# Triangle attention followed by a window scan: score, bias and maximum in one VectorE operation, and a projection in another PSUM bank

## The chip, the cores and the metric

The kernel runs on one core of a Trainium2 chip. The metric is the device time of one execution in microseconds (us); a lower time is better. The engines of the core work from queues of their own, each in order, and wait for each other by semaphores: TensorE (PE: matrix products and transposes, results into PSUM), VectorE (DVE), ScalarE (ACT), GpSimd (POOL) and SyncE (SP: issues the DMAs). SBUF and PSUM are the on-chip memories[...].

## The reference

Two layers work on an image of 256 x 256 positions with 128 channels, in float32. Each is added to its own input: `x = x + layer(group_norm(x))`. Layer 1 (convolution, windowed selective scan, gated projection) is not edited here. Layer 0 is attention along each of the 256 rows, with four heads of 32 channels:

```python
xn = (x - mu) * jax.lax.rsqrt(var + EPS) * ln_w + ln_b
tri_bias = jnp.einsum('bijd,dh->bhij', xn, w_tri)[:, None]
mask_bias = INF * (mask[:, :, None, None, :] - 1.0)
q = (xn @ w_q).reshape(B, I, J, H, C) * (1.0 / np.sqrt(C))
...
scores = jnp.einsum('bimhc,binhc->bihmn', q, k) + tri_bias + mask_bias
attn = jax.nn.softmax(scores, axis=-1)
o = jnp.einsum('bihmn,binhc->bimhc', attn, v)
g = jax.nn.sigmoid((xn @ w_g + b_g).reshape(B, I, J, H, C))
o = (g * o).reshape(B, I, J, H * C)
return o @ w_o + b_o
```

For every row and head the scores are a 256 x 256 matrix: a product of queries and keys plus a bias that is the same for all rows (tri_bias) plus a mask bias.

## The kernel before

The program has three stretches. The first computes statistics and normalised input (`xn_d`) and the bias `tri_d`. The second is the attention loop. The third is layer 1: a scan with its own schedule, which begins with `group_norm(1)` and so needs the statistics of all pairs of the second.

The attention loop takes the rows in 128 pairs of 512 tokens. One step of the loop is one row; even and odd steps alternate, and the order of all work in a step is written out by hand (under a manual schedule, L553 to L641), so the order of these calls is the order of each engine's queue. In step s the loop works on several rows at once:

- `now` (row s): its scores, made in the step before, get their bias and maximum and are exponentiated.
- `mid` (row s-2): its exponentials are transposed on PE (`turn`), 128 x 128 at a time, and copied out of PSUM (`turn_out`), one head by VectorE, one by ScalarE.
- `old` (row s-3): its transposed exponentials meet the values in `mix`, giving o_p.
- `nxt` (row s+1): its scores are computed by PE.
- pairs `ahead`, `behind`, `done`: queries, keys and values of the next pair; gate and softmax shares of the last; output projection of the one before that.

What each name does, with its engine:

- `scores` (L455 to L468, PE): sc0 and sc1, two PSUM tiles of two banks each, one for two heads. A tile has four blocks of 128 x 256: two heads by two halves of the query positions.
- `bias` (L446, GpSimd): tm, tri bias plus mask, 128 x 2048 per row, two steps ahead.
- `add` (L470, VectorE): `at` = scores + tm for the four blocks of a tile at once, 128 x 1024.
- `peak` (L478, VectorE): nmax, the negative maximum of each block, over 128 x 1024.
- `exps` (L484, ScalarE): `exp(at + nmax)` in place, one operation per block, its sums into den.
- `invert` and `widen` (L496, L500): the reciprocals of den (VectorE), spread out by GpSimd.
- `queries`, `keys`, `values`, `gates`, `shares`, `project`: PE products into the one-bank tile that `side0` (L337) hands out, tag m. The pool has one such buffer, so a product waits until the one before it has been read out.
- `queries_out` (L366), `keys_out` (L374), `values_out` (L389): read out on ScalarE. `gates_out` (L397), `shares_out` (L415), `project_out` (L426): on VectorE. The last writes xr, which `store` (L431) puts into the statistics and sends to memory.
- `gather` (L418, VectorE): og, the product of o_p with the gate.
- o_p (L535) has a PSUM bank of its own. sc0 and sc1 take four banks, the transposes two, tag m one, o_p one[...].

`logistic` (L129) is the sigmoid of the gate, three ScalarE operations, each on the last one's result.

Of the kernel before, what the change touches and what calls it, by code (L numbers as in the profile page):

```python
# [12 lines left out]
F32 = mybir.dt.float32  # L13
AF = mybir.ActivationFunctionType
ALU = mybir.AluOpType
AX = mybir.AxisListType
# [3 lines left out]
P = 128  # L20
# [4 lines left out]
HC = 32  # L25
# [42 lines left out]
def kernel(  # L68
# [28 lines left out]
    nc = tc.nc  # L97
# [31 lines left out]
    def logistic(e):  # L129

        nc.scalar.activation(e, e, AF.Exp, scale=-1.0)
        nc.scalar.activation(e, e, AF.Ln, bias=one)
        nc.scalar.activation(e, e, AF.Exp, scale=-1.0)
# [34 lines left out]
    for dh in range(2):  # L168
        nc.scalar.dma_start(
            out=wtap[:, dh], in_=conv_w[:, dh * P : (dh + 1) * P].rearrange("t d -> d t")  # L170
# [5 lines left out]
    for dh in range(2):  # L176
        for k in range(KD):
            o, back = k % 2, k // 2
            for at, lo, n in (
# [5 lines left out]
                    out=wx[:, dh, o, at : at + n],  # L185
# [4 lines left out]
    for back in range(2):  # L190
        at = 32 * back
        nc.scalar.dma_start(
            out=wdt[at : at + DTR], in_=dt_w[:, 2 * back : 2 * back + 2]
        )
        for o in range(2):
            for dh in range(2):
                j = 2 * (o + 2 * back) + dh
                nc.scalar.dma_start(
                    out=wdt[at + DTR : at + DTR + 1, o, dh * P : (dh + 1) * P],
# [61 lines left out]
    with tc.tile_pool(name="lnc", bufs=1) as cp, tc.tile_pool(  # L261
        name="lnx", bufs=3
    ) as xp, tc.tile_pool(name="lnt", bufs=3) as tp, tc.tile_pool(
        name="lnp", bufs=2, space=PSUM
# [9 lines left out]
        for k in range(KD):  # L274
            for nh in range(2):
                for blk in range(NBLK):
                    nc.scalar.dma_start(
                        out=bdiag[k][nh][blk].rearrange("p t n -> p (t n)"), in_=zero
# [33 lines left out]
    with tc.tile_pool(name="atc", bufs=1) as cp, tc.tile_pool(  # L312
        name="atx", bufs=7
    ) as xp, tc.tile_pool(name="att", bufs=3) as tp, tc.tile_pool(
        name="ats", bufs=8
    ) as wp, tc.tile_pool(name="atps", bufs=1, space=PSUM) as ps_s, tc.tile_pool(
        name="atpt", bufs=1, space=PSUM
    ) as ps_t, tc.tile_pool(name="atpm", bufs=1, space=PSUM) as ps_m, tc.tile_pool(
        name="atpo", bufs=1, space=PSUM
# [11 lines left out]
        for mc in range(2):  # L331
            nc.sync.dma_start(
                out=trib[:, :, mc, :],
# [3 lines left out]
        def side0(name):  # L337
            return ps_m.tile([P, 512], F32, name=name, tag="m")

        class Pair:  # L340
# [24 lines left out]

            def queries_out(self):  # L366
                self.qs = tp.tile([P, 512], F32, name="qs")
                nc.scalar.mul(self.qs, self.q_p, 1.0 / math.sqrt(HC))

            def keys(self):  # L370
                self.k_p = side0("k_p")
# [48 lines left out]
                nc.vector.tensor_mul(self.og, self.o_p, self.gate)  # L420

            def project(self):
                self.y_p = side0("y_p")
                nc.tensor.matmul(self.y_p, wo, self.og, start=True, stop=True)

            def project_out(self):  # L426
# [8 lines left out]
        class Row:  # L435
# [32 lines left out]
                        )  # L468

            def add(self, hp):  # L470
                self.at[hp] = wp.tile([P, 4, IMG], F32, name="at")
                nc.vector.tensor_add(  # L472
                    self.at[hp],
                    self.sc[hp].rearrange("p h m n -> p (h m) n"),
                    self.tm[:, 4 * hp : 4 * hp + 4],
                )

            def peak(self, hp):  # L478
                self.nmax[hp] = wp.tile([P, 4], F32, name="nmax")
                nc.vector.tensor_reduce(  # L480
                    self.nmax[hp], self.at[hp], AX.X, ALU.max, negate=True
                )

            def exps(self, hp, js):  # L484
                if hp == 0 and js[0] == 0:
                    self.den = wp.tile([P, NH, 2], F32, name="den")
                for j in js:
                    nc.scalar.activation(  # L488
                        self.at[hp][:, j, :],
                        self.at[hp][:, j, :],  # L490
                        AF.Exp,
                        bias=self.nmax[hp][:, j : j + 1],
                        accum_out=self.den[:, 2 * hp + j // 2, j % 2 : j % 2 + 1],
                    )

# [36 lines left out]
            def mix(self):  # L532
                pair = self.pair
                if self.r == 0:
                    pair.o_p = ps_o.tile([P, 512], F32, name="o_p")  # L535
                for n in range(2):
                    for h in range(NH):
                        base = h * HC
                        nc.tensor.matmul(
                            pair.o_p[base : base + HC, self.row],  # L540
                            pair.vs[:, self.r, n, base : base + HC],
                            self.aT[h][:, n, :],
                            start=(n == 0),
                            stop=(n == 1),
                        )
# [4 lines left out]
        def pick(items, i):  # L550
            return items[i] if 0 <= i < len(items) else None

        with tc.manual_schedule():  # L553
            for pair in pairs[0:4]:
                pair.load()
            first = pairs[0]
            first.mask_bias()
            rows[0].bias()
            rows[1].bias()
            first.queries()  # L560
            first.queries_out()
            first.keys()
            first.keys_out()
            rows[0].scores()
            first.values()
            first.values_out()
            for s in range(n_rows + 4):
                sg, odd = divmod(s, 2)
                now, nxt, mid, old = (
                    pick(rows, s),  # L570
                    pick(rows, s + 1),
                    pick(rows, s - 2),
                    pick(rows, s - 3),
                )
                ahead, behind, done = (
                    pick(pairs, sg + 1),
                    pick(pairs, sg - 1),
                    pick(pairs, sg - 2),
                )
                if not odd:  # L580
                    if sg + 4 < n_pairs:
                        pairs[sg + 4].load()
                    if behind:
                        behind.load_residual()
                    if ahead:
                        ahead.mask_bias()
                if s + 2 < n_rows:
                    rows[s + 2].bias()
                if old:
                    old.mix()  # L590
                if now:
                    now.add(0)
                    now.peak(0)
                if mid:
                    mid.turn(0)
                if now:
                    now.exps(0, [0])
                if done:
                    if odd:
                        done.project_out()  # L600
                    else:
                        done.gather()
                if mid:
                    mid.turn_out(0)
                if now:
                    now.exps(0, [1, 2, 3])
                if odd and ahead:
                    ahead.keys()
                    ahead.keys_out()
                if not odd and behind:  # L610
                    behind.gates()
                    behind.gates_out()
                if now:
                    now.add(1)
                if mid:
                    mid.turn(1)
                    mid.turn_out(1)
                if now:
                    now.peak(1)
                if odd and behind:  # L620
                    behind.shares()
                    behind.shares_out()
                if not odd and ahead:
                    ahead.queries()
                    ahead.queries_out()
                if now:
                    now.exps(1, [0, 1, 2, 3])
                if nxt:
                    nxt.scores()
                if odd and ahead:  # L630
                    ahead.values()
                    ahead.values_out()
                if not odd and done:
                    done.project()
                if odd and done:
                    done.store()
                if not odd and behind:
                    logistic(behind.gate)
                if 0 <= s - 1 < n_rows:
                    rows[s - 1].invert()  # L640
                    rows[s - 1].widen()  # L641
# [648 lines left out]
    with tc.manual_schedule():  # L1290
# [37 lines left out]
        for i, unit in enumerate(units):  # L1328
            j, place = divmod(i, per_job)
# [102 lines left out]
```

## Time and profile before

| | |
|---|---|
| median of 3 runs | 24110.36 us (24109.98 to 24111.08) |
| profiled execution, device time | 24104.07 us |
| its span, first to last instruction | 24102.3 us |
| granted TensorE clock, mean | 0.993 |
| instructions | 423533 |
| PE, VectorE, ScalarE, GpSimd busy | 95%, 91%, 77%, 88% of the span |
| first and last sum of scores and bias (L472) | 541.6 and 2718.0 us |

The busy shares are means over the whole span, and most of that is layer 1, so they say little of the attention loop, which lies between about 541 and 2720 us. In groups of instructions, a row gives source line, engine, operation, the tiles written and read (buffer numbers left out), their shapes and the count; behind the bar the busy time in us and the mean duration of one in ns; behind the second bar the engine's idle time just before them and what ended most of it. Busy time counts overlapping instructions once, so it can be less than the count times the mean. In a table of waits, a row gives who waited, for whom, the total in us, how many times, and the longest. In a timeline, a row gives the start, the length, engine, line and operation. Matrix products are pipelined and their ends are modelled.

### The profile page before, as it was taken

What the parts mean: (1) busy time and instruction counts of PE and PEld (TensorE: products, weight loads), DVE (VectorE), ACT (ScalarE), POOL (GpSimd) and SP (SyncE); (2) the same over time, 40 slices, a digit from 0 to 9 for tenths busy, and PEclk for the clock granted to TensorE, in tenths of its full rate; (3) what the DMA queues carried; (4) which work ended last, traced back from release to release, by engine and by line L of the source; (5) the groups of instructions that cost most, each with busy time, mean ns of one, the idle gap of its engine ahead of it and who ended that gap; (6) DMA issues with size and microseconds to landing.
All of it is one profiled execution on the core that took longest, in us unless ns stands there. A gap on an engine that the chain in (4) does not pass through costs nothing.

```text
span 24102.3 us, 423533 instructions
## 1 busy us (share of the span) xinstructions
PE 22947.3 (95%) x171020; PEld 17081.0 (71%) x171020; DVE 22036.1 (91%) x14740; ACT 18625.8 (77%) x35334; POOL 21291.6 (88%) x5966
## 2 busy tenths in 40 slices
PE   7888899999999999999999999999999999999999
PEld 2555577777777777777777777777777777777777
DVE  6888899999999999999999999999999999999998
ACT  5777777777777777777777777777777777777776
POOL 3666699999999999999999999999999999999999
PEclk9999999999999999999999999999999999999999
DMA  5222244444444444444444444444444444444444
GB/s 195 64 62 62 93 159 160 157 159 161 159 160 158 159 160 160 160 158 159 160 161 159 159 158 160 160 160 160 158 159 160 160 160 158 159 160 160 160 159 147
DMA packets 2000298, 3638.51 MB, mean 151 GB/s; under 512 B 1129584, under 2 KB 1131760, under 8 KB 1725824
## 3 DMA queue, kind: packets, MB, share of 16 engines
q1 hardware_dynamic: 1985616, 3602.35, 43.4%
q8 instruction: 1346, 22.05, 0.4%
q10 hardware_dynamic: 12720, 9.07, 0.1%
q14 instruction: 616, 5.05, 0.1%
HBM read 3467.33 MB, written 143.65 MB: 150 GB/s over the span
## 4 chain that ended last, share of the span: by engine, by line
PE 60%; DVE 23%; issue 7%; ACT 7%; DMA 2%; SPq 1%; POOL 0%; ACTq 0%; POOLq 0%; DVEq 0%
PE b_p L1180 22%; PE y_p L1218 19%; DVE h L1200 18%; PE dt_p L1017 4%; PE cv_p L768 4%; ACT at L488 2%; PE xd_p L948 2%; PE dut_p L1051 2%; PE in_p L719 1%; ACT da L1167 1%; DMA res<-x_d 1%; PE sc L462 1%; DVE dt L1033 1%; PE v_p L381 1%; DVE nmax L480 1%
## 5 line engine op out<-in xcount | busy, mean ns | idle before, releaser
L1207 POOL TENSOR_TENSOR h<-h,cc 128x2048 f32<-128x2048 f32 x4096 | 18591.8, 4549 | 1460.5 <-POOL h L1207 544.8
L1200 DVE TENSOR_TENSOR_SCAN h<-da,b_p 128x1024 f32<-128x1024 f32 x8192 | 18228.9, 2270 | 1417.8 <-PE b_p L1180 1384.6
L1167 ACT ACTIVATE da<-dt,am 128x508 f32<-128x508 f32 x16384 | 10396.2, 706 | 1236.5 <-DVE h L1200 1223.9
L1180 PE MATMUL b_p<-diag,dut 64*128 64x256 f32 x65536 | 8594.4, 395 | 622.9 <-DVE h L1200 559.3
L1218 PEld LDWEIGHTS y_p<-ident,h 128*128 128x128 f32 x65536 | 7141.4, 140 | 1412.9 <-issue 1386.7
L1218 PE MATMUL y_p<-ident,h 128*128 128x128 f32 x65536 | 8003.9, 275 | 5.9 <-POOL h L1207 5.9
L1180 PEld LDWEIGHTS b_p<-diag,dut 64*128 64x128 f32 x65536 | 5852.3, 186 | 2946.7 <-DVE h L1200 1353.8
L736 ACT ACTIVATE tap<-xin,wtap 128x512 f32<-128x512 f32 x2048 | 1432.3, 743 | 0.0
L1040 POOL TENSOR_TENSOR du<-dt,u 128x512 f32<-128x512 f32 x1024 | 1307.4, 1277 | 58.9 <-DMA z<-bt 56.0
L768 PE MATMUL cv_p<-ident,tap 128*128 128x128 f32 x9216 | 1225.6, 274 | 5.1 <-DVE xct L785 3.7
L1158 ACT ACTIVATE da<-ident 128x16 f32<-128x16 f32 x1536 | 347.9, 227 | 1140.8 <-DVE h L1200 1140.8
L488 ACT ACTIVATE at<-at,nmax 128x256 f32<-128x256 f32 x2048 | 1019.4, 502 | 237.8 <-DVE nmax L480 237.8
L449 POOL TENSOR_TENSOR tm<-trib,mb 128x2048 f32<-128x2048 f32 x256 | 1166.3, 4556 | 10.7
L768 PEld LDWEIGHTS cv_p<-ident,tap 128*128 128x128 f32 x9216 | 1047.6, 141 | 170.1 <-issue 161.5
L1027 ACT ACTIVATE sp<-dt_p 128x512 f32<-128x512 f32 x1024 | 602.4, 588 | 728.3 <-PE dt_p L1017 728.2
L1017 PE MATMUL dt_p<-xd,wdt 9*128 9x512 f32 x2048 | 1151.1, 641 | 2.5 <-DVE dt L1033 2.2
L1060 ACT COPY dut<-dut_p 128x512 f32<-128x512 f32 x1024 | 586.6, 573 | 473.0 <-PE dut_p L1051 473.0
L503 POOL COPY wide<-rden 128x256 f32<-128x256 f32 x256 | 101.5, 396 | 826.8 <-DVE rden L498 824.9
L1028 ACT ACTIVATE sp<-sp,one 128x512 f32<-128x512 f32 x1024 | 743.0, 726 | 33.4
L516 PEld LDWEIGHTS aT_p<-ident,at 128*128 128x128 f32 x4096 | 451.0, 141 | 343.0 <-issue 142.6
L1033 DVE SCALAR_TENSOR_TENSOR dt<-sp,dt_p 128x512 f32<-128x512 f32 x1024 | 677.8, 662 | 16.0 <-DMA z<-bt 11.3
L472 DVE TENSOR_TENSOR at<-sc,tm 128x1024 f32<-128x1024 f32 x512 | 613.5, 1198 | 56.5 <-POOL wide L503 30.8
(132 smaller groups left out, 16368.0 us busy)
## 6 DMA issues: line engine op xcount, KB each, us to landing
cc<-c_d SPq DMA_DIRECT2D x2048, 1024.0 KB
diag<-z SPq DMA_DIRECT2D x1024, 1024.0 KB
xt<-in_x_dram SPq DMA_DIRECT2D x16, 2048.0 KB
xt<-in_x_dram SPq DMA_DIRECT2D x32, 1024.0 KB
xn_d<-xn SPq DMA_DIRECT2D x32, 1024.0 KB
xn<-xn_d SPq DMA_DIRECT2D x128, 256.0 KB
mb<-in_mask_dram SPq DMA_DIRECT2D x128, 256.0 KB
xr<-in_x_dram SPq DMA_DIRECT2D x128, 256.0 KB
```

The source lines that it names most:

```text
L449: nc.gpsimd.tensor_add(self.tm, trib.rearrange("p h m n -> p (h m) n"), self.pair.mb[:, self.row].unsqueeze(1).to_broadcast([P, 2 * NH, IMG]),
L488: nc.scalar.activation(self.at[hp][:, j, :], self.at[hp][:, j, :], AF.Exp, bias=self.nmax[hp][:, j : j + 1], accum_out=self.den[:, 2 * hp ...
L736: nc.scalar.activation(scaled.rearrange("p s (y x) -> p s y x", x=WIN), self.xin[:, dh] .rearrange("p y f x -> p (y f) x")[:, 2 * dy : 2 * ...
L768: nc.tensor.matmul(cv_p[:, s], one_tap[:, s], ident, start=(t == 0 and s == 0), stop=(t == 8 and s == GS - 1), is_transpose=True, skip_gro ...
L1017: nc.tensor.matmul(token_order(self.dt_p), wdt[rows, self.o, dh * P : (dh + 1) * P], token_blocks(self.xd[rows]), start=True, stop=True,)
L1033: nc.vector.scalar_tensor_tensor(dt, self.sp, CEIL, self.dt_p, ALU.min, ALU.max)
L1040: nc.gpsimd.tensor_mul(token_blocks(du), token_order(self.dt[back][dh]), token_blocks(self.u[:, dh]),)
L1167: nc.scalar.activation(da[:, :, j, lo:hi], dt[:, :, lo:hi], AF.Exp, scale=am[:, a0 : a0 + 1])
L1180: nc.tensor.matmul(b_p[:, s, :, h * 64 : (h + 1) * 64].rearrange("p n t -> p t n"), job.dut[self.back][rows, p, h, self.dh * P : (self.dh ...
L1200: nc.vector.tensor_tensor_scan(out=out_, data0=d0, data1=d1, initial=0.0, op0=ALU.mult, op1=ALU.add)
L1207: nc.gpsimd.tensor_mul(self.pair, self.pair, cc.rearrange("p n s t -> p s n t"))
L1218: nc.tensor.matmul(job.y_p[:, 2 * p + s, self.dh * P : (self.dh + 1) * P], self.h[:, s, j], ident, start=(first and s == 0 and j == 0), st ...
```

## The change

Six edits, all in the attention loop:

1. `add` and `peak` become one. Instead of a 128 x 1024 addition and a 128 x 1024 reduction for each tile, four `tensor_tensor_reduce` operations per tile each handle one 128 x 256 block: they write at = -(scores + tm) and fold the minimum of it into the block's column of nmax. In the compiled order each is two VectorE instructions, one of 128 x 256 and one that writes 128 x 1. `peak` is gone, and nmax of sc1 is made where `add(1)` stood, ahead of the second transposes' copy.
2. `exps` takes scale -1 to undo the sign.
3. `queries_out` moves from ScalarE to VectorE.
4. The projection y_p takes its tile from o_p's pool, with a common tag o, and no longer from tag m.
5. `project` and `project_out` move: `project` from the end of the even step to behind the queries of the same step; `project_out` from the odd step after it to right behind `project`.
6. `keys` and `keys_out` move from the odd step to the end of the even step ahead of it, behind the next row's scores and ahead of `logistic`. `shares` (the PE part) moves up in the odd step, ahead of the second transposes.

```diff
             def queries_out(self):
                 self.qs = tp.tile([P, 512], F32, name="qs")
-                nc.scalar.mul(self.qs, self.q_p, 1.0 / math.sqrt(HC))
+                nc.vector.tensor_scalar(
+                    self.qs, self.q_p, 1.0 / math.sqrt(HC), None, ALU.mult
+                )
...
             def project(self):
-                self.y_p = side0("y_p")
+
+                self.y_p = ps_o.tile([P, 512], F32, name="y_p", tag="o")
                 nc.tensor.matmul(self.y_p, wo, self.og, start=True, stop=True)
...
             def add(self, hp):
+
                 self.at[hp] = wp.tile([P, 4, IMG], F32, name="at")
-                nc.vector.tensor_add(
-                    self.at[hp],
-                    self.sc[hp].rearrange("p h m n -> p (h m) n"),
-                    self.tm[:, 4 * hp : 4 * hp + 4],
-                )
-
-            def peak(self, hp):
                 self.nmax[hp] = wp.tile([P, 4], F32, name="nmax")
-                nc.vector.tensor_reduce(
-                    self.nmax[hp], self.at[hp], AX.X, ALU.max, negate=True
-                )
+                for j in range(4):
+                    nc.vector.tensor_tensor_reduce(
+                        out=self.at[hp][:, j],
+                        in0=self.sc[hp][:, j // 2, j % 2],
+                        in1=self.tm[:, 4 * hp + j],
+                        scale=-1.0,
+                        scalar=3.0e38,
+                        op0=ALU.add,
+                        op1=ALU.min,
+                        accum_out=self.nmax[hp][:, j : j + 1],
+                    )
...
                         bias=self.nmax[hp][:, j : j + 1],
+                        scale=-1.0,
...
-                    pair.o_p = ps_o.tile([P, 512], F32, name="o_p")
+                    pair.o_p = ps_o.tile([P, 512], F32, name="o_p", tag="o")
...
                     now.add(0)
-                    now.peak(0)
                 if mid:
                     mid.turn(0)
                 if now:
                     now.exps(0, [0])
-                if done:
-                    if odd:
-                        done.project_out()
-                    else:
-                        done.gather()
+                if done and not odd:
+                    done.gather()
                 if mid:
                     mid.turn_out(0)
                 if now:
                     now.exps(0, [1, 2, 3])
-                if odd and ahead:
-                    ahead.keys()
-                    ahead.keys_out()
+                if odd and behind:
+                    behind.shares()
                 if not odd and behind:
                     behind.gates()
                     behind.gates_out()
...
                     mid.turn(1)
                     mid.turn_out(1)
-                if now:
-                    now.peak(1)
                 if odd and behind:
-                    behind.shares()
                     behind.shares_out()
                 if not odd and ahead:
                     ahead.queries()
                     ahead.queries_out()
+                if not odd and done:
+                    done.project()
+                    done.project_out()
                 if now:
                     now.exps(1, [0, 1, 2, 3])
...
                 if odd and ahead:
                     ahead.values()
                     ahead.values_out()
-                if not odd and done:
-                    done.project()
+                if not odd and ahead:
+                    ahead.keys()
+                    ahead.keys_out()
```

Layer 1 and the first stretch are word for word the same. In each pair of rows VectorE gets 16 blocks of the new operation where it had four additions and four reductions, and one operation more for the queries; ScalarE has one fewer; PE, GpSimd and the DMA queues have the same instructions as before, PE's in another order.

## Prediction
> **What bounds the kernel now.** I read the busy time by stage first, then the VectorE groups of the stage that the change touches, then its waits, then a timeline of one pair of image rows for the steps from start to start. The first table gives busy time by stretch (us, then each engine's busy time and instructions in brackets).
>
> ```profile
> core 0: us, PE busy (x) PEld busy (x) DVE busy (x) ACT busy (x) POOL busy (x), PEclk, DMA share, GB/s
> 0.00:541.00 541.00, 381.75 (x796) 105.54 (x796) 334.34 (x655) 292.67 (x518) 140.22 (x136) 0.96 0.59 213
> 541.00:2720.00 2179.00, 1871.07 (x14743) 1124.15 (x14736) 1927.09 (x2416) 1730.58 (x5355) 1336.33 (x637) 0.96 0.21 61
> 2720.00:24102.00 21382.00, 20694.52 (x155491) 15851.32 (x155489) 19774.64 (x11670) 16602.60 (x29462) 19815.03 (x5194) 1.00 0.46 159
> ```
>
> The reader is to see that the attention loop of layer 0 is the second line, 2179 of 24102 us. Layer 1, the third line, holds no edited line and starts only after layer 0 has ended (its group norm needs all statistics), so whatever the loop gains or loses arrives in full and nothing else moves. The loop has 128 pairs: 2179/128 = 17.02 us a pair. Per pair VectorE is busy 15.06 us, PE 14.62, ScalarE 13.52, GpSimd 10.44. VectorE is the fullest and still idles 1.96 us. Its groups in that stretch:
>
> ```profile
> L480 DVE TENSOR_REDUCE nmax<-at 128x4 f32<-128x1024 f32 x512 | 621.7, 1214 | 8.8
> L472 DVE TENSOR_TENSOR at<-sc,tm 128x1024 f32<-128x1024 f32 x512 | 613.5, 1198 | 56.5 <-POOL wide L503 30.8 <-PE sc L462 24.4 <-POOL mb L360 1.2
> L528 DVE COPY aT<-aT_p 128x512 f32<-128x512 f32 x508 | 346.9, 683 | 0.3 <-PE aT_p L516 0.3
> L416 DVE TENSOR_TENSOR gate<-gate,rd_p 128x512 f32<-128x512 f32 x126 | 86.6, 687 | 168.1 <-PE rd_p L409 168.1
> ```
>
> The first two, the sum and the maximum over it, are what the change replaces: (621.7 + 613.5)/128 = 9.65 us of the 15.06. The idle time sits before L416. The waits (600 to 2700 us) say why:
>
> ```profile
> ACT at L488 <- DVE nmax L480: 230.7, 246, 1.2
> PE rd_p L409 <- ACT ks L376: 170.9, 123, 1.4
> DVE gate L416 <- PE rd_p L409: 162.8, 123, 1.6
> ACT vs L391 <- PE v_p L381: 141.2, 123, 2.1
> PE k_p L372 <- DVE xr L427: 76.4, 123, 0.6
> ```
>
> This is one ring over three engines: the exponentials wait for a whole maximum, ks stands behind them on ScalarE, rd_p waits for ks (same PSUM bank, tag m), VectorE waits for rd_p. Each pair loses 162.8/123 = 1.32 us there.
>
> [...]
>
> **The price of the new operation.** Rows nearest to it (whole-run groups), and two timelines:
>
> ```profile
> L230 DVE COPY permt<-pt_p 128x256 f32<-128x256 f32 x1 | 0.4, 424 | 0.0
> L223 DVE COPY perm<-ident 128x2 f32<-128x2 f32 x128 | 9.0, 159 | 0.0
> L1200 DVE TENSOR_TENSOR_SCAN h<-da,b_p 128x1024 f32<-128x1024 f32 x8192 | 18228.9, 2270 | 1417.8 <-PE b_p L1180 1384.6
> ```
>
> ```profile
> 1809.98 0.19 DVE L498 RECIPROCAL rden<-den 128x8 f32<-128x8 f32 x1
> 1810.09 1.17 DVE L472 TENSOR_TENSOR at<-sc,tm 128x1024 f32<-128x1024 f32 x1
> 1811.30 1.22 DVE L480 TENSOR_REDUCE nmax<-at 128x4 f32<-128x1024 f32 x1
> ...
> 1816.47 0.57 ACT L376 COPY ks<-k_p 128x512 f32<-128x512 f32 x1
> 1816.93 0.58 ACT L530 COPY aT<-aT_p 128x512 f32<-128x512 f32 x1
> ```
>
> A 128x256 read of PSUM lasts 424 ns. Independent neighbours overlap by about 0.08 us (in the same timelines a 0.69 us operation is followed after 0.61), so from start to start the main costs 0.34. The smallest operations follow each other every 9.0/128 = 0.07 us. A block is then 0.34 + 0.07 = 0.41 us: my value. Upper bound without a slower rate: no overlap, 0.424 + 0.159 = 0.58. [...]
>
> **The change part by part, per pair.**
> - Four adds and four reduces go: -9.65 us of VectorE. Sixteen blocks come: 16 * 0.41 = 6.56.
> - qs moves from ScalarE (L368, 597 ns; 0.47 from start to start, as between the two ScalarE lines above) to VectorE: +0.61, and ScalarE -0.47.
> - Everything else on VectorE stays: four aT copies 2.44, gate 0.67, og 0.60, the product with rd_p 0.60, statistics 0.61, xr 0.67, two reciprocals at 0.11: 5.81. New VectorE sum 6.56 + 0.61 + 5.81 = 12.98 against 15.06.
> - ScalarE: 13.52 - 0.47 = 13.05. Each exponential now needs one block, not an add and a reduce: its first wait shrinks from 2.4 to about 0.5 us, so the 230.7 us row should nearly vanish.
> - PE's work is the same. From start to start in the timeline: two mixes 2.0, four groups of transposes 4.0, g 0.87, q 1.06, y 1.05, two score groups 2.21, k 0.96, rd 0.56, v 1.09: 13.8 us. It becomes the fullest engine.
> - y_p goes into the bank of o_p (allocated in L535; tag o). Bank m then carries five tenants a pair, g, q, k, rd, v, not six. New wait: the first mix of an odd step waits for xr (L427) on VectorE. Behind it on PE stand the transposes, rd_p, the scores. xr ends about 4.5 us after g_p, that mix can start after k_p at about 5.4, so it is covered by 0.9 us; uncovered it would cost at most xr's 0.75.
> - project_out follows y_p in the same even step: VectorE meets it after qs (0.6 us), PE has issued y_p a full 2 us earlier. k_p moves to the end of the even step and must wait for qs; ks then stands before the sigmoid's three ScalarE operations (L131 to L133, 1.9 us in a row), which start later. rd_p moves ahead of the second transposes, so the product with rd_p finds it done: the 162.8 us row goes.
> - Queues of SP and GpSimd keep their order; GpSimd's 10.44 us a pair leaves it ahead.
>
> What is late next: the ring k_p -> ks -> sigmoid -> eight exponentials and two aT copies of the odd step -> vs -> g_p -> ... -> k_p. ScalarE's part: handoff 0.1, ks 0.5, sigmoid 1.9, eight exponentials at 0.49 = 3.9, two copies 0.9, vs 0.6, handoff 0.1: 8.0. PE from g_p: g 0.9, transposes 1.0, q 1.1, y 1.05, scores 1.1, k 1.0: 6.2. Ring 14.2 us. Laying the three queues beside it I find one wait more that nothing covers: the second head of an odd step's transposes waits for aT1's copy on ScalarE, about 0.4, and some 0.4 of handoffs that PE can't hide. So 14.2 + 0.8 = 15.0 us a pair. Gain 17.02 - 15.0 = 2.0, times 127 steady pairs = 257 us. The profiled execution took 24104.07 (span 24102.3 and 1.8 around it): 24104 - 257 = 23847. The median of the runs shown is 6 us above the profiled one, so 23853, rounded 23855.
>
> **The rivals.**
> 1. The block costs 0.58. VectorE: 6.42 + 16 * 0.58 = 15.7, with 0.6 of stalls 16.3: gain 0.7 * 127 = 90, 24020. For it: operations this short were never back to back here. Against: the 0.07 step of L223. Chance 0.13.
> 2. The handoffs eat more: sigmoid behind ks, mix behind xr, each hop twice what I took, 16.2 a pair: gain 105, 24005. For it: before the change three engines at 80 to 88% cost 1.96 us above the fullest. Chance 0.09.
> 3. Slower: [...] Then 6.42 + 16 * 0.75 = 18.4 and 0.6 of stalls: 19.0, +2.0 * 127 = +254, 24360. It decides from a block of (17.02 - 0.6 - 6.42)/16 = 0.62 us on. For it: [...]no row shows the new one. [...] Chance 0.20.
> 4. No change: block near 0.62, gain and loss cancel. Chance 0.06.
>
> **How the numbers follow.** Mine has 0.52, with its own range of 14.3 (the ring alone) to 15.8: 23765 to 23955. Faster by over 0.2% (48 us, about what a measurement can tell from no change) is mine, 1 and 2: 0.74; the same 0.06; slower 0.20. The range starts at 23765 and runs over 1, 2 and 4 to 24160, which leaves out most of rival 3.
>
> **What would show it.** The new group near 0.41 us from start to start; the row ScalarE on nmax under 60 us; VectorE before the product with rd_p near nothing; a PE busy share of the loop over 90%; the loop's end near 2465 us, layer 1 unchanged. I am wrong if a block takes over 0.62 us, or if the mix waits for xr in most pairs.

## The result and the profile after

The changed kernel took 23746.35 us (median of four runs, 23741.51 to 23748.33), against 24110.72 for the kernel before (four runs): a ratio of 0.9848, 95% interval 0.9831 to 0.9865. That is 364 us less; 257 were forecast, and the time lies 19 us below the range. The profiled execution took 23741.51 us with a span of 23739.7.

The gain lies in the attention loop. Busy time by stretch after the change, columns as in the table of before:

```profile
core 0: us, PE busy (x) PEld busy (x) DVE busy (x) ACT busy (x) POOL busy (x), PEclk, DMA share, GB/s
541.00:2350.00 1809.00, 1735.95 (x14687) 1067.43 (x14686) 1529.37 (x5593) 1631.62 (x5212) 1335.21 (x635) 1.00 0.25 73
...
2380.00:23739.00 21359.00, 20677.46 (x155392) 15852.13 (x155390) 19760.08 (x11648) 16593.53 (x29438) 19814.36 (x5189) 1.00 0.47 159
```

The loop ends earlier (its last step on VectorE, the gathering of the statistics in L141, starts at 2371.07 us and not at 2734.94: 363.9 us), and layer 1 takes what it took. PE is now busy 96% of the loop, VectorE 85% and ScalarE 90%. PE still waits, so it is the fullest engine and not a full one. The clock column now reads 1.00, where the loop of before had 0.96.

VectorE's groups in the loop (560 to 2330 us), the new operation first:

```profile
L478 DVE CUSTOM_DVE_ANT_0 at<-sc,tm 128x256 f32<-128x256 f32 x1988 | 716.5, 417 | 0.2 <-issue 0.2
L534 DVE COPY aT<-aT_p 128x512 f32<-128x512 f32 x497 | 341.1, 686 | 132.9 <-PE aT_p L522 132.7
L478 DVE DVE_READ_ACCUMULATOR2_ANT nmax<- 128x1 f32 x1988 | 165.5, 83 | 0.0
L418 DVE TENSOR_TENSOR gate<-gate,rd_p 128x512 f32<-128x512 f32 x125 | 84.6, 677 | 0.0
```

and in order of time:

```profile
1499.75 0.69 DVE L534 COPY aT<-aT_p 128x512 f32<-128x512 f32 x1 [1.07 <-PE aT_p L522]
1500.36 0.41 DVE L478 CUSTOM_DVE_ANT_0 at<-sc,tm 128x256 f32<-128x256 f32 x1
1500.70 0.08 DVE L478 DVE_READ_ACCUMULATOR2_ANT nmax<- 128x1 f32 x1
1500.70 0.42 DVE L478 CUSTOM_DVE_ANT_0 at<-sc,tm 128x256 f32<-128x256 f32 x1
1501.04 0.08 DVE L478 DVE_READ_ACCUMULATOR2_ANT nmax<- 128x1 f32 x1
1501.04 0.42 DVE L478 CUSTOM_DVE_ANT_0 at<-sc,tm 128x256 f32<-128x256 f32 x1
1501.39 0.08 DVE L478 DVE_READ_ACCUMULATOR2_ANT nmax<- 128x1 f32 x1
```

The 128x256 instruction of a block, its main, lasts 417 ns, and the read of its accumulator, the 128x1 one (83 ns), starts at the same instant as the next main. A block is 0.345 us from start to start, as much as the prediction gave to the main alone (0.34), so the read costs nothing here. The slower rate that rival 3 feared isn't there: the 128x512 copy is followed after 0.61 us, so by an estimate from these two intervals 256 elements fewer take 0.61 - 0.345 = 0.265 us less, 0.97 elements a nanosecond, where the scan (L1200) takes 2270 ns for 1024, 0.45 a nanosecond. The idle time before the product with rd_p (L418) is gone. The waits of the loop (600 to 2300 us, 120 pairs) are others now:

```profile
ACT ks L378 <- PE k_p L374: 156.9, 120, 1.3
DVE aT L534 <- PE aT_p L522: 128.5, 120, 1.1
...
PE aT_p L522 <- ACT aT L536: 67.1, 120, 0.6
DVE og L422 <- PE o_p L545: 65.1, 119, 0.5
```

No exponential waits for a maximum any more. ScalarE and VectorE wait for PE. The only wait of PE's products for another engine is the third row, 67.1/120 = 0.56 us a pair, in the odd step.

### The profile page after: what moved, and what is told of

It reads as the page before. It is cut to its first block, busy times and chain, and to the rows that moved or that the text cites. A ratio compares the mean times of both kernels' runs of the same rounds, so it can differ in the third digit from the quotient of the medians.

```text
span 23739.7 us, 426729 instructions
## 1 busy us (share of the span) xinstructions
PE 22815.3 (96%) x171020; PEld 17037.2 (72%) x171020; DVE 21644.3 (91%) x17940; ACT 18532.3 (78%) x35206; POOL 21292.8 (90%) x5966
## 4 chain that ended last, share of the span: by engine, by line
PE 64%; DVE 21%; issue 7%; ACT 5%; DMA 2%; SPq 1%; POOL 0%; ACTq 0%; POOLq 0%; DVEq 0%
PE b_p L1182 22%; PE y_p L1220 19%; DVE h L1202 18%; PE dt_p L1019 4%; PE cv_p L770 4%; PE xd_p L950 2%; PE dut_p L1053 2%; PE aT_p L522 1%; PE in_p L721 1%; ACT da L1169 1%; DMA res<-x_d 1%; PE sc L465 1%; DVE dt L1035 1%; PE q_p L364 1%; PE v_p L383 1%
## 5 line engine op out<-in xcount | busy, mean ns | idle before, releaser
L478 DVE CUSTOM_DVE_ANT_0 at<-sc,tm 128x256 f32<-128x256 f32 x2048 | 738.0, 417 | 7.4 <-PE sc L465 5.7
L1053 PE MATMUL dut_p<-ident,du 128*128 128x128 f32 x4096 | 644.5, 280 | 3.5 <-DVE dt L1035 2.3
```

The source lines that it names most:

```text
L1053: nc.tensor.transpose(self.dut_p[:, h * DI + dh * P : h * DI + (dh + 1) * P], self.du[back][dh][:, (2 * h + p) * P : (2 * h + p + 1) * P], ...
```

## Two kinds of pairs before the change

The start of GpSimd's wide copies, one per row, shows how long a pair takes. In the kernel before (every second one, from the timeline):

```profile
1784.95 0.40 POOL L503 COPY wide<-rden 128x256 f32<-128x256 f32 x1 [4.22 <-DVE rden L498]
...
1801.39 0.40 POOL L503 COPY wide<-rden 128x256 f32<-128x256 f32 x1 [4.22 <-DVE rden L498]
...
1819.44 0.40 POOL L503 COPY wide<-rden 128x256 f32<-128x256 f32 x1 [4.22 <-DVE rden L498]
```

One pair took 16.44 us, the next 18.05. Between 1500 and 2000 us 11 of 29 pairs are of the long kind (17.5 to 18.1 us); the others take 16.3 to 16.9. The mean of the pairs from 600 to 2300 us is 17.06. The prediction starts from 17.02, the length of the loop over 128, and no pair takes that. Small stretches of the same trace show what happens at the border:

```profile
1796.00:1798.00 2.00, 1.40 (x9) 0.78 (x7) 2.00 (x3) 2.00 (x9) 1.17 (x1) 1.00 0.91 283
1798.00:1800.00 2.00, 0.87 (x8) 0.74 (x12) 0.73 (x2) 2.00 (x8) 0.00 (x0) 0.95 0.75 215
1800.00:1802.00 2.00, 2.00 (x17) 1.24 (x14) 1.44 (x4) 1.44 (x6) 0.53 (x2) 0.50 0.05 20
1802.00:1804.00 2.00, 2.00 (x20) 1.71 (x23) 1.97 (x2) 0.43 (x1) 1.92 (x2) 0.70 0.04 12
```

The third column from the right is the granted clock. Behind PE's wait for ks (first busy column: 0.87 of 2 us) it falls to 0.50 for about 0.2 + 2.0 + 1.2 = 3.4 us (in windows of 0.2 us it reads 0.50 or 0.52 from 1799.8 to 1803.2), and the scores and v_p in it take 2.04 and 1.88 us. In the pair before, at a clock of 1.00, they take 1.15 and 1.16 (from 1783.25 and 1784.33 us). PE's timeline there, with its idle time in brackets:

```profile
1795.18 1.12 PE L372 MATMUL k_p<-xn,wk 128*128 128x512 f32 x2 [0.62 <-DVE xr L427]
1796.14 0.60 PE L516 MATMUL aT_p<-ident,at 128*128 128x128 f32 x4
1797.08 0.66 PE L516 MATMUL aT_p<-ident,at 128*128 128x128 f32 x4 [0.34 <-ACT aT L530]
1799.13 0.63 PE L409 MATMUL rd_p<-ident,wide 128*128 128x128 f32 x4 [1.39 <-ACT ks L376]
1799.68 2.04 PE L462 MATMUL sc<-ks,qs 32*128 32x256 f32 x16
1801.66 1.88 PE L381 MATMUL v_p<-wv,xn 128*128 128x128 f32 x8
```

From 1500 to 2000 us the clock falls 11 times, each time for 3.4 us (in windows of 0.5 us), as often as there are long pairs. What brings it down isn't shown by this trace. PE was idle for 0.62, 0.34 and 1.39 us ahead of the fall shown, with work between, and from 1796.14 to 1799.68 us, 3.54 us, it had only transposes. But the pair before has the same three waits (ahead of 1778.75, 1780.65 and 1782.69 us), and its clock stays at 1.00. Over the loop (600 to 2300 us, 100 pairs) they come to 62.1, 34.0 and 138.9 us, 0.62, 0.34 and 1.39 a pair, and only two of five pairs are long: the lengths repeat every five pairs for the most part (16.43, 16.43, 18.03, 16.70 and 17.75, together 85.3 us). In the changed kernel every pair of the same 500 us takes 14.25 us, and the clock stays at 1.00.

## Experiments

Each time is the median of four or five executions, with the kernel before on the same chip beside it (24110 to 24112 us). The loop's time per pair is read as above, from the wide copies.

**The blocks alone.** The kernel before with this edit and the sign in `exps`:

```diff
             def add(self, hp):
...
-                nc.vector.tensor_add(
+                for j in range(4):
+                    nc.vector.tensor_tensor_reduce(
...
-            def peak(self, hp):
```

> The kernel before with the one-operation blocks alone; order, banks and the engine of qs stay as before. Theory A (the time came from VectorE's sum and from the short first wait of the exponentials): VectorE falls from 15.1 to 5.8 + 16*0.345 = 11.3 us a pair, PE (13.7) is next, and about 0.9 us of waits for ks and xr stay: 14.6 us a pair, 24110 - 128*2.4 = 23800. Rival B (the moves and the bank carry the gain, since the ring over ks and rd_p stays): 16.0 us a pair or more, 23980 or above.

Measured: 23870.0 us, ratio 0.99 (0.9883 to 0.9916), 15.24 us a pair. It is nearer to A than to B and misses both figures. In this window (1000 to 2000 us, 65 pairs) the ring over ks is still there:

```profile
DVE gate L416 <- PE rd_p L409: 104.2, 65, 1.6
PEld rd_p L409 <- issue: 103.7, 65, 1.6
PE rd_p L409 <- ACT ks L376: 90.2, 65, 1.4
```

PE waits 1.39 us a pair for ks as it did before, and all pairs are alike: the clock stays at 1.00 in this kernel. So the wait for ks alone didn't bring the clock down here; PE's other two waits of before (0.62 and 0.34 us) are gone, since PE is busy 909.81 of 1000 us and the 90.2 us above are all of its idle time.

**The moves alone.** The changed kernel with the addition and the reduction of before inside `add`:

> The changed kernel with the 128x1024 addition and the 128x1024 reduction instead of the blocks; all moves, the bank and qs on VectorE stay. Theory A: VectorE has 9.65 + 0.6 + 5.8 = 16.1 us a pair and bounds it: 16.1 to 16.7, so 23990 to 24070. Rival B (the moves carry the gain): 15.0 us or less, below 23860.

Measured: 23950.28 us, ratio 0.9933 (0.9918 to 0.9948), 15.81 us a pair. VectorE is busy 991 of 1000 us: it bounds, as A said, 0.3 us a pair below A's figure. A took the sums of durations, and neighbours overlap (by about 0.08 us, a 0.69 us operation being followed after 0.61). Against the short pairs of before (16.43 us) a pair gains 0.62: of the 160 us 0.62*128 = 79 came from the order of the queues and the rest from the clock, which stays at 1.00 here as well.

**PE's gap filled, in the kernel before.** In the odd step, ahead of `shares`, the products of `mix` are issued a second time with the same values:

```diff
                 if odd and behind:
+                if odd and old:
+                    old.mix_again()
+                if odd and behind:
                     behind.shares()
```

> The kernel before with the eight matrix products of one mix per pair issued a second time, with the same values, in PE's wait for ks ahead of rd_p (odd steps): 1.0 us more PE work a pair in a wait of 1.39 us. Theory G (before, PE's long wait lets the granted clock fall to 0.5 for some 3.4 us in about two of five pairs, which makes those pairs 18.0 us and not 16.43; with the wait filled the clock stays): faster although it does more, 24110 - 128*0.59 = 24035. Rival H (the 18.0 us pairs have another cause and the lower clock follows from it): 24110 or up to 30 us more.

Measured: 24033.71 us, ratio 0.9967 (0.9954 to 0.998). With about 1.0 us of products more in each pair the kernel is 78 us faster, pairs take 16.43 us without a long one among them, and the clock column reads 0.99 over the loop:

```profile
541.00:2660.00 2119.00, 1933.22 (x16892) 1125.87 (x16892) 1926.79 (x2431) 1733.10 (x5375) 1339.00 (x640) 0.99 0.23 63
```

G holds, H falls: with the gap filled the low clock and the long pairs go together, and the slow scores and v_p above show how the clock makes them long. What brings the clock down isn't settled: fused_only keeps a wait of 1.39 us in each pair, y_in_m (below) one of 1.45, and the clock's mean over the whole run is 0.997 in both, as in the changed kernel, where the kernel before has 0.993.

**The sigmoid ahead of ks.** The changed kernel with:

```diff
+                if not odd and behind:
+                    logistic(behind.gate)
                 if not odd and ahead:
                     ahead.keys()
                     ahead.keys_out()
...
-                if not odd and behind:
-                    logistic(behind.gate)
```

> The changed kernel with the three sigmoid operations of the even step ahead of ks instead of behind it on ScalarE. Theory C (the ring k_p, ks, sigmoid, one exponential, the aT copy, PE's second transposes sets the 14.25 us): the sigmoid runs in the 1.3 us for which ScalarE waits for k_p, PE's wait of 0.56 us a pair goes, PE alone bounds with 13.7: 23746 - 128*0.56 = 23675. Rival D (PE's queue or VectorE sets the pace and that wait only stands where a later one would): 23730 to 23750. Rival E (ks 0.56 us later delays rd_p and the scores): slower, 23780 or more.

Measured: 23715.95 us, ratio 0.9836 (0.9821 to 0.9851), 14.0 us a pair. PE's wait for the aT copy is gone, so C named the right ring; but only 30 of the 72 us came. What stands behind it is seen in PE's timeline:

```profile
1503.29 1.48 PE L465 MATMUL sc<-ks,qs 32*128 32x256 f32 x16
1504.93 1.13 PE L383 MATMUL v_p<-wv,xn 128*128 128x128 f32 x8 [0.16 <-DVE gate L418]
```

The scores of the odd step hold PE for 1.48 us, not 1.1, and v_p waits 0.16 more for VectorE's product with rd_p. The third score product overwrites sc1, whose blocks VectorE takes only after the aT0 copy, for which it waits; that product stands behind them in VectorE's queue. The next run tests this.

**Three blocks ahead of the aT0 copy**, in odd steps, on top of the last edit:

```diff
                 if now:
                     now.add(0)
+                    if odd:
+                        now.add(1, [0, 1, 2])
...
                 if now:
-                    now.add(1)
+                    now.add(1, [3] if odd else range(4))
```

> The kernel with the sigmoid ahead of ks, and in odd steps three of the four blocks of sc1 ahead of the aT0 copy on VectorE. Theory C' (after the sigmoid's move the next wait is PE's third score product, 0.3 us a pair, for blocks that stand behind VectorE's wait for the transposes): PE alone bounds with 13.7 us a pair, 23716 - 128*0.3 = 23678. Rival D (the wait moves to the aT0 copy's reader): 23710 to 23730.

Measured: 23653.59 us, ratio 0.981 (0.9795 to 0.9825), 13.47 us a pair. That is 62 us less than the last run, more than the 38 that C' gave: C' took 0.3 us a pair, and the two holds of PE above are 1.64 - 1.1 = 0.54. It is the fastest kernel of the study, 93 us below the changed one. PE has no gap left:

```profile
1000.00:2000.00 1000.00, 1000.00 (x8607) 626.06 (x8604) 901.35 (x3260) 953.22 (x3044) 778.70 (x371) 1.00 0.28 79
```

**One more ScalarE copy, in the ring and out of it.** Two kernels, each the changed one with the same additional 128x256 copy per pair; in the first ahead of the odd step's exponentials, in the second ahead of `keys` in the even step:

```diff
+                    spare = tp.tile([P, IMG], F32, name="spare")
+                    nc.scalar.copy(spare, trib[:, 0, 0, :])
```

> The changed kernel with one ScalarE copy of 128x256 (about 0.4 us, to a tile that nobody reads) per pair, in the odd step ahead of its first exponential, between sigmoid and aT copy. Theory C (ring k_p, ks, sigmoid, exponential, aT copy, PE): the full 0.4 is paid, 23746 + 128*0.4 = 23797. Rival I (the ring that the prediction named, over vs and g_p, with 0.3 us to spare): 23760 or less.

> The same additional ScalarE copy, but in the even step ahead of ks, where ScalarE waits 1.3 us for k_p. Theory C: nothing, 23746 within 10 us. Rival I (any ScalarE work counts): 23797.

Measured: 23788.91 and 23751.22 us. The same work costs 43 us in one place and 5 in the other. In the second ScalarE's busy time rises from 902 to 923 of 1000 us, 0.30 us a copy (expected were 0.4). In the first PE's idle time grows from 0.56 to 0.86 us a pair (1000 - 940.36 = 59.64 us in 69 pairs), and a pair takes 14.56 us, 0.31 more. So the ring of theory C sets the changed kernel's pace, and ScalarE's sum doesn't.

**qs back on ScalarE.**

```diff
-                nc.vector.tensor_scalar(
-                    self.qs, self.q_p, 1.0 / math.sqrt(HC), None, ALU.mult
-                )
+                nc.scalar.mul(self.qs, self.q_p, 1.0 / math.sqrt(HC))
```

> The changed kernel with qs read out by ScalarE, as before the change. Theory C: ScalarE's 0.5 us falls into its wait for k_p of 1.3 us and VectorE has slack: 23746 within 10 us. Rival F (ScalarE's sum matters, its move was needed): 0.47*128 more, 23805.

Measured: 23745.36 us. It makes no difference, as C said.

**One more VectorE operation per row.** The changed kernel with, ahead of `invert`:

```diff
+                if now:
+                    spare = tp.tile([P, 512], F32, name="spare")
+                    nc.vector.tensor_scalar(spare, now.pair.xn, 1.0, None, ALU.mult)
```

> The changed kernel with one VectorE operation more per row, 128x512 to a tile that nobody reads, ahead of the reciprocals: 0.4 us from start to start, 0.8 a pair, nearly the 16*0.065 = 1.0 by which the prediction overpriced the blocks. Theory C: VectorE idles over 2 us a pair, so nothing, 23746 within 10 us: the block's price didn't decide the miss. Rival J (the cheaper block is where the unforecast gain came from): 0.8*128 more, 23850.

Measured: 23752.8 us; VectorE's busy time rises from 846 to 890 us in 1000 (0.62 us a pair, not the 0.8 expected; one lasts 412 ns), and the pairs still take 14.25 us. J falls as far as VectorE's sum goes. That a dearer block in its own place would have cost nothing isn't shown by this run; for it speaks that no exponential waits for a maximum.

**y_p back in tag m**, at its new place:

```diff
-                self.y_p = ps_o.tile([P, 512], F32, name="y_p", tag="o")
+                self.y_p = side0("y_p")
```

> The changed kernel with y_p back in tag m, at its new place right behind the queries. Theory K (o's bank is what lets the projection stand there): y_p then waits on PE until VectorE has read q_p out, 1.6 us after it could have started, all behind it waits too: up to 23746 + 128*1.6 = 23950. Rival L (the bank doesn't matter): 23746 within 10 us.

Measured: 23962.25 us, 216 more than the changed kernel and 12 above K's limit. L falls, and K's wait is there. In 63 pairs (1000 to 2000 us):

```profile
PE y_p L427 <- DVE qs L368: 91.1, 63, 1.4
DVE xr L430 <- PE y_p L427: 76.9, 63, 1.2
```

PE waits 1.45 us a pair for the bank, and xr after it is late in turn. By the times of the two kernels a pair takes 14.25 + 216/127 = 15.95 us.

**keys and rd_p back at their old places**, all else changed:

```diff
+                if odd and ahead:
+                    ahead.keys()
+                    ahead.keys_out()
-                if odd and behind:
-                    behind.shares()
...
                 if odd and behind:
+                    behind.shares()
                     behind.shares_out()
...
-                if not odd and ahead:
-                    ahead.keys()
-                    ahead.keys_out()
```

> The changed kernel with keys, their copy and rd_p's products back at their old places in the odd step; blocks, bank, projection and qs stay changed. Theory M (rd_p waits for ks behind the odd step's exponentials again, over 1 us a pair): 15.0 us a pair, 23746 + 128*0.75 = 23842. Rival N (that move is worth little once the blocks are in): below 23775.

Measured: 23788.62 us, 14.56 a pair. This expectation missed: the move is worth 42 us, between M's 96 and N's limit of 29. PE does wait for ks, 67.9/69 = 0.98 us a pair, but it no longer has the 0.56 us wait for the aT copy, and the two exchange. The weight loads of the odd step's first mix, which k_p no longer stands ahead of, wait for xr as well (38.9/68 = 0.57 us). Why only 0.31 us a pair remains of this isn't followed up here. The wait for ks (1000 to 2000 us):

```profile
PE rd_p L411 <- ACT ks L378: 67.9, 69, 1.0
```

The runs put in a row, each one step from the last, give the parts of the 17.06 - 14.25 = 2.81 us a pair:

| step | us a pair after it | gain |
|---|---|---|
| before, mean of 600 to 2300 us | 17.06 | |
| clock kept at 1.00 (short pairs) | 16.43 | 0.63 |
| blocks (fused_only) | 15.24 | 1.19 |
| projection and its bank, qs on VectorE (keys_old) | 14.56 | 0.68 |
| keys and rd_p moved (the change) | 14.25 | 0.31 |

The parts depend on the order: taken first, all moves together gain 0.62 beside the clock.

## Why the prediction was right and wrong

**The direction, the place and what goes away** were right. The loop alone changed, PE became the fullest engine, the waits for nmax and for rd_p went, and VectorE's sum fell below PE's. Neither of the prediction's two signs of being wrong came: the miss is in what is late next.

**PE's work** was nearly right: 13.8 us forecast, 14.25 - 0.56 = 13.69 outside its wait in the changed kernel, and 13.47 in split_blocks, where PE has no gap.

**The block's rate** was right, its price a little high: 0.41 us against 0.345, because the accumulator's read lies wholly beside the next block. Rival 3's 0.75 us a block was its author's estimate; the nearest that the traces show is the scan, 2270 ns where the addition takes 1198 for as many elements. VectorE's sum is no term of the 15.0, so 1.0 us a pair too much in it didn't enter the forecast. Rivals 1, 3 and 4 hung on a price of 0.58 or more and fell with it.

**The step that failed** is "So 14.2 + 0.8 = 15.0 us a pair". The ring of 14.2 went from k_p over ks, the sigmoid, all of the odd step's exponentials and vs to g_p. In the trace g_p doesn't wait for vs, which ends 0.33 us before it starts, so that ring takes 14.25 - 0.33 = 13.92 us and doesn't bind. On top of that ring the prediction put 0.4 for the wait of the second head's transposes for the aT copy, and 0.4 of handoffs. The wait is real (0.56), but it isn't a delay of that ring: it closes a ring of its own, k_p, ks, sigmoid, one exponential, aT copy, PE from there to the next k_p. Two rings through the same k_p compete, and the longer one sets the pace. One turn of it, from the timelines of PE and ScalarE, with vs and g_p of the other ring:

```profile
1511.25 1.13 PE L374 MATMUL k_p<-xn,wk 128*128 128x512 f32 x2
1512.41 0.59 ACT L378 COPY ks<-k_p 128x512 f32<-128x512 f32 x1 [1.30 <-PE k_p L374]
1512.89 0.63 ACT L131 ACTIVATE gate<-gate 128x512 f32<-128x512 f32 x1
...
1514.85 0.49 ACT L493 ACTIVATE at<-at,nmax 128x256 f32<-128x256 f32 x1
1515.35 0.56 ACT L536 COPY aT<-aT_p 128x512 f32<-128x512 f32 x1
1515.96 0.66 PE L522 MATMUL aT_p<-ident,at 128*128 128x128 f32 x4 [0.56 <-ACT aT L536]
...
1519.75 0.56 ACT L393 COPY vs<-v_p 128x512 f32<-128x512 f32 x1
1520.64 1.02 PE L397 MATMUL g_p<-xn,wg 128*128 128x512 f32 x2
...
1525.50 1.13 PE L374 MATMUL k_p<-xn,wk 128*128 128x512 f32 x2
```

From k_p's start to the transposes' start are 4.71 us, from there to the next k_p, in which PE has no idle time, 9.54: together the 14.25 us of a pair. The runs act_in_ring, act_off_ring and sigmoid_first show that this ring is the one that sets the pace. For the 0.4 of handoffs the trace shows no place: the ring was summed from intervals from start to start and had 0.1 us for each crossing already. No run tests this part by itself. With the 0.8 left out, (17.02 - 14.2)*127 = 358 us would have been forecast, near the 364 measured; but that would have been luck in part, since the ring summed there isn't the one that binds.

**The sizes** add up so: of the 107 us between forecast and measured, 0.75*127 = 95 are the pace of 15.0 against 14.25, 5 the mean of 17.06 against 17.02, 3 the 128th pair, and 4 the start and the end of the loop. The low end of the range, 23765, came from the ring alone, taken as 14.3; the pairs took less than that.

**What it did not see.** It took all of VectorE's 1.96 us of idle time a pair for waits that the order of the queues makes. Some 0.6 us of its 17.02 were the clock's, in two of five pairs. The base of its sum was a mean that held this cost, and its 15.0 held none, so this part of the gain was counted without being named, which was luck; had the changed kernel kept the clock's falls, the same sum would have been wrong. The signs lay in views that it quoted: a clock of 0.96 in the loop's row beside 1.00 in layer 1's.

**Rival 2** (handoffs at double price, 24005) had the sign of the handoffs wrong. **The bank** was priced as covered by 0.9 us for the mix behind xr, and that was right: xr ends at 1510.69 + 0.74 = 1511.43 us, and k_p holds PE until the mix starts at 1512.31, 0.88 us later. What the bank is for, y_p not waiting for the copy of the queries, was not worked out, and is worth 1.7 us a pair (y_in_m).

## What to carry to other kernels

When the order of the queues closes several rings, the longest sets the time: a wait in one of them must not be added to the length of another, and each needs its own sum from start to start. Look at the granted clock in stretches as short as the loop's step before trusting a mean per step, since it can hide slow stretches: in this loop, with gaps of 0.62, 0.34 and 1.39 us on TensorE in each pair, the clock stood at 0.50 for about 3.4 us behind them in two of five pairs, and 1.0 us of products in the longest gap made it 78 us faster (before_fill). Work on an engine that isn't the fullest is free or not by its place in the order: the same copy cost 43 us between two links of a ring and 5 us where its engine waited anyway.

## What the runs showed of the hardware

- A tensor_tensor_reduce (add, then minimum) of 128x256 float32, one source in PSUM and one in SBUF, lasts 417 ns and follows its like after 0.345 us; its accumulator read (83 ns) adds nothing between them.
- The TensorE clock fell to half for about 3.4 us at a time in a loop where PE was busy 86% of the time, with gaps of 0.62, 0.34 and 1.39 us within 4.6 us; with 1.0 us of products in the longest gap (before_fill) it was 0.99 over the loop. With a gap of 1.39 us in each pair and without the other two (fused_only) it was 1.00.
